# A fused two-layer graph network kernel: the order of the last transition (third norm, tiles held, first tiles of the last layer)

## The chip, the cores and the metric

The kernel runs on one core of one Trainium2 chip. A core has a matrix engine (TensorE, PE in the profile), three engines for elementwise work (VectorE or DVE, ScalarE or ACT, GpSimd or POOL) and a queue engine that issues transfers (SyncE or SP). Each takes its instructions strictly in the order in which they were written, and waits on semaphores where an operand or a buffer comes from another engine. The metric is the device time of one execution in microseconds, lower is better.

## What is computed

Two layers over a batch of 8 graphs with 2048 nodes and 256 features, all sharing one adjacency matrix. Cut to what matters:

```
# layer 0: attention in 8 chunks of 256 keys, 4 heads of 64, softmax within each chunk, chunks summed
q, k, v = x @ Wq.T + bq, x @ Wk.T + bk, x @ Wv.T + bv
scores  = clip(q . k / 8, -10, 10), and -10 where adj == 0
ctx     = sum over chunks of softmax(scores) @ v
a       = layernorm(ctx @ Wo.T + bo + x) * gamma + beta
x1      = layernorm(x + a)

# layer 1: graph attention, 4 heads of 64
Wh      = x1 @ W
e       = leaky_relu(s_src[i] + s_dst[j], 0.2), and -inf where adj == 0
h       = elu(softmax_j(e) @ Wh)
out     = layernorm(x1 + h)
```

Everything is float32; the masks are kept as 8-bit values.

## The kernel before

The kernel walks the graphs b = 0 to 7. For each it runs layer 0 in 64 slots (4 query blocks of 512 nodes, 2 pairs of heads, 8 chunks), taken two at a time in 32 "pairs" (p = 0 to 31). In the same loop it runs layer 1 of the graph before (`lower`), so that the matrix products of one layer cover the elementwise work of the other. The order on every engine is written by hand; no scheduler moves anything.

**A pair of layer 0.** PE makes four blocks of scores (`unit`, L425, tile `ps`), VectorE clips and masks each (`evict`, L444, tile `pr`), ScalarE takes exp (`exps`, L467), PE multiplies by the values (`product`, L478, tile `pc`), ScalarE copies out (L485), and VectorE and GpSimd normalise and add up (`normalize`, L495 to L504).

**A tile of layer 1.** Each graph has 128 tiles: 8 units (2 halves of the rows, 4 heads) of 16 blocks of nodes. `make` produces one tile of weights `e` with one VectorE instruction (L927), out of a row of source factors, a column `gd` and a mask tile; `use` multiplies it into the accumulators `pa` on PE (L964). A pair with layer 1 beside it uses four tiles. `make` runs two tiles ahead of `use`. A tile of `e` takes a buffer from a pool named in `lower.room`, or from the list `lower.extra` of places that happen to be free (parts of `h1`, `qT`).

**Closing a unit.** After 16 tiles ScalarE copies `pa` out (L986), and `close` carries on in steps that `rest(n)` advances: maximum and reciprocal on VectorE (L1007, L1008), a product on GpSimd (L1013, for the last units) or ScalarE (L1019), exp and relu on ScalarE (L1024, L1025), and a combination on VectorE into `h1` (L1029).

**The last graph, b = 7.** Two things differ. First, layer 1 of graph 6 does not run out with the pairs: the last `LATE` slots (12, so six pairs) run alone, and 24 tiles are held back, to be used one by one in the transition. In the lone pairs one tile each is made ahead (four, from p = 27 on, and one more in the last pair). Second, after the transition layer 1 of graph 7 runs with nothing beside it (`alone`). There every third tile (k % 3 == 2, `by_pool`) is made by ScalarE (L888, L889) and GpSimd (L890) instead of VectorE, up to nine tiles ahead (`make_ahead`), and the rest by VectorE. ScalarE copies the row of each unit to PSUM (`lift`, L856). `weigh` (L777, GpSimd) scales the features of one head.

**The transition** is the list `order` near the end of the graph loop. Work on the nodes is done in four groups of 512 (`Between`). When the pairs end, the third group (`before`) still needs its second norm, and the fourth (`group`) everything: context transposes (`ctx`, L528, L531), output matmuls (`steps[1]`, L631), addition (`steps[2]`, L642), first norm (`group.a`, L545 to L557 and L594), scale and addition (`steps[5]`, L648, L651), second norm (`b2`), store, transposes (`turn_all`, L334, L337) and values (L673, L680, L684). The third group's second norm runs as `again` (L651), `sums` and `squares` on ScalarE (L563, L575), `factors` (four small steps on GpSimd, L587 to L590), `finish` (four applies L594 and a store L656 on ScalarE's queue), transposes and values. Then the factors of the last layer: `fs[0]` maximum (L740, L742, L744), `fs[1]` spread (L748, L755 to L762), `fs[2]` rows (L767, L770, L771, L772, L777), and `coming.start`, which broadcasts the row with 16 matmuls (L786). In the list, `M` makes a tile, `U` uses one, `R` advances a closing by one step; they fill the places where PE would otherwise wait.

SP issues the masks of each tile (`et`, L863), the slabs (L413), the group inputs, and in the transition the 2 MB of masks for the first half of the last layer (L825). Row factors (`srow`, L222) are issued in four pieces, one with each `make`, while layer 1 runs beside a pair, and at once otherwise.

Of the kernel before, what the change touches and what calls it, by code (L numbers as in the profile page):

```python
# [18 lines left out]
CH = 512  # L19
# [3 lines left out]
def adj_resnorm_kernel(  # L23
# [19 lines left out]
    nc = tc.nc  # L43
# [26 lines left out]
    PAIRS = SLOTS // 2  # L70
# [2 lines left out]
    FIRST = [sum(BANKS[:m]) for m in range(len(BANKS))]  # L73
    TILES = len(UNITS) * NT
    STEP = TILES // SLOTS
    LATE = 12
    WIDE = max(BANKS)
    AHEAD_E = 5
    AHEAD_P = 8
# [42 lines left out]
    qT = big.tile([P, KC, N], F32, tag="qT", name="qT")  # L122
# [285 lines left out]
    spare, lone = [1], []  # L408
# [281 lines left out]
    every = tuple(range(QT))  # L690
# [106 lines left out]
    class Layer1:  # L797
# [71 lines left out]
            return self.edge.pop(k)  # L869

        def by_pool(self, k):
            return self.alone and k % 3 == 2

        def make_ahead(self, k):

# [284 lines left out]
    for g in range(NCH):  # L1160
        _, _, keys, values, queries = groups[g]
# [67 lines left out]
    lower = None  # L1229
    for b in range(B):  # L1230
# [8 lines left out]
        group = before = None  # L1239
        for p in range(PAIRS):  # L1240
            s0, s1 = 2 * p, 2 * p + 1
            q, i = p // QP, p % QP
            along = lower if b + 1 < B or s0 < SLOTS - LATE else None
            if b + 1 == B and not along:

                lone[:] = [
                    qT[:, 0, : 2 * CH].rearrange("p (k n) -> p k n", k=2),
                    h1[:, :QT, :].rearrange("p (k t) f -> p k (t f)", k=2),
                ]
                if p == PAIRS - 4:  # L1250
                    lower.extra = [
                        h1[:, QT : 2 * QT, :].rearrange("p t f -> p (t f)"),
                        qT[:, 1, : 2 * CH],
                        qT[:, :, 2 * CH : 3 * CH],
                    ]
            more = p + 1 < PAIRS
            slow[0] = bool(along) and more
            if not slow[0]:
                drip(len(pieces))

            def hook(now, later):
                if group and i in now:
                    now[i](group)
                if before and i in later:
                    later[i](before)

            if p + 2 < PAIRS:
                load_slab(p + 2)
            if i == 0 and q:
                before, group = group, Between(b, q - 1, sd, waug)  # L1270
            if p == PAIRS - 2 and b + 1 < B:
                turns = [project(b + 1, g) for g in range(NCH)]
                turns[0].pop(0)()

            ending = b + 1 == B and not more
            if ending:
                room = kT[:, 0, : QT * F].rearrange("p (t f) -> p t f", f=F)
                last = Between(b, NCH - 1, sd, waug, room)

            hook(FIRST_OF, {})  # L1280
            if i == QP - 1 and q > 1:
                turn_context(q, 0)
            if p:
                normalize(s0 - 1)
            if more:
                us = units_of(p + 1)
                waiting = burst(p + 1)
                evict(*waiting[0][0], waiting[0][1])
                exps(*us[0])
                exps(*us[1])  # L1290
            if along:
                along.rest(1)
                along.make()
                along.use()
                along.make()
            else:
                if more:
                    evict(*waiting[1][0], waiting[1][1])
                    exps(*us[2])
                if not lower and masks.left():  # L1300
                    masks.step()
            if ending:
                last.bias()
                lower.room = prp, "pr"
                lower.make()
            hook(MIDDLE_OF, NEXT_MIDDLE)
            for each in closings:
                each.do(p, "add", "factors")
            if i == 2 and q:
                turn_context(q - 1, 1)  # L1310
            if i == QP - 2 and q < 2:
                turn_context(q, 0)
            product(s0)
            send()
            for each in closings:
                each.do(p, "load")
            if i == 1 and q:
                load_context(b, q - 1, 1)
            if i == QP // 2 + 1:
                load_context(b, q, 0)  # L1320
            if along:
                normalize(s0)
                if more:
                    for us_ps in waiting[1:]:
                        evict(*us_ps[0], us_ps[1])
            elif more:
                evict(*waiting[2][0], waiting[2][1])
                exps(*us[3])
                if lone and p >= PAIRS - 5:
                    lower.rest(1)  # L1330
                    lower.make()
            if i == 0 and q:
                send_context(b, q - 1, 1)
            if i == QP // 2:
                send_context(b, q, 0)
            if along:
                if more:
                    exps(*us[2])
                along.rest(1)
                along.use()  # L1340
                along.make()
                along.use()
                along.make()
                along.use()
            elif ending:
                lower.use()
                normalize(s0, nc.vector)
            else:
                normalize(s0)
                if not lower and masks.left() and (p < QP - 2 or p % 2 == 0):  # L1350
                    masks.step()
            if p == PAIRS - 1 and not ending:
                turns[0].pop(0)()
                group.again()
            product(s1)
            if along and more:
                exps(*us[3])
            hook(LAST_OF, NEXT_LAST)
            hook(FINALLY_OF, NEXT_FINALLY)
            for each in closings:  # L1360
                each.do(p, "sums", "squares", "finish")
# [4 lines left out]
        before = group  # L1366
        gd, fs = factors(b, sd, waug)
        group = None
# [8 lines left out]
        coming = Layer1(b, gd, waug)  # L1377
# [8 lines left out]
        def group_shift():  # L1386
            group.shift()

        early = [
            lambda: before.b2.stats(every),  # L1390
            lambda: None,
            lambda: before.finish(),
            lambda: before.load(ep.tile([P, KC, CH], F32, tag="e", name="x1t") if b + 1 < B else None),
            lambda: before.turn(),
            lambda: before.values((0, 1), parts),
            lambda: before.values((2, 3), parts),
        ]
# [13 lines left out]
        if b + 1 < B:  # L1411
            (k0, v0, q0), (l1, t1, k1, v1, q1), (l2, t2, k2, v2, q2), (l3, t3, k3, v3, q3) = turns
            rest = [lambda: lower.rest(1)] if lower else []
            order = [begin, early[0], *rest, l1, k0, ctx, early[2], v0, steps[0], *rest, steps[1], t1, l2, *rest]
            order += [q0, steps[2], early[3], steps[3], l3, k1, *rest, steps[4], v1, early[4], t2, q1]
            order += [steps[5], k2, steps[6], early[5], early[6], steps[7], coming.begin, v2, t3]
            order += [lambda: [load_slab(p) for p in range(2)], steps[8], steps[9]]
            order += [lambda: k3(fs[0]), fs[1], lambda: q2(fs[2]), coming.start, v3, start_next]
            order += [lambda: [exps(*us) for us in units_of(0)], q3, coming.make, coming.make]
        else:  # L1420


            M, U, R = lower.make, lower.use, lambda: lower.rest(1)
            b2 = lambda: before.b2
            order = [begin, U, U, U, ctx, before.again, M, lambda: b2().sums(every), U, steps[1], M]
            order += [steps[2], lambda: group.a.stats(every), lambda: b2().squares(every)]
            order += [lambda: b2().factors(nc.gpsimd), U, U, U, M, U, M, U, early[2], steps[4]]
            order += [before.turn_all, lambda: coming.load_masks(0), group_shift, M, U, early[5], early[6]]
            order += [steps[5], M, U, R, M, U, M, U, R, steps[6], M, U, steps[7], M, U, R, M, U, steps[8]]
            order += [M, U, steps[9], R, M, U, M, U, R, M, U, fs[0], M, U, fs[1], M, U, fs[2], U]  # L1430
            order += [lambda: coming.start(fs[4])]
            assert sum(p is U for p in order) + 1 == LATE * STEP
            assert sum(p is M for p in order) + 2 + 1 + 4 >= LATE * STEP
        for piece in order:
            send()
            piece()
# [6 lines left out]

    closing, ending = Closing(B - 2, CLOSING_ALONE), Closing(B - 1, ENDING)
    weigh = fs[3]
    for _ in range(STEP):
        lower.make()
    for s in range(SLOTS):
# [55 lines left out]
```

## Time and profile before

| | us |
|---|---|
| median of 3 runs (3559.84 to 3566.21) | 3564.57 |
| the profiled execution, its own time | 3559.92 |
| its span in the profile | 3558.1 |
| PE busy in it | 3499.2 |
| pairs 26 to 31 of the last graph (3297.95 to 3347.45) | 49.50 |
| transition (3347.45 to 3397.46) | 50.01 |
| first 12 tiles of the last layer (3397.46 to 3419.72) | 22.26 |
| the other tiles of the last layer (3419.72 to 3544.30) | 124.58 |

The last four rows are read from PE's timeline: the stages end where the first matmul of the next one starts. Times inside the execution are counted from the start of the span. In the views of single engines a row gives start, length, engine, source line, operation and tiles, the number of instructions merged into the row (x), and in brackets the idle time before it with the instruction that ended it.

### The profile page before, as it was taken

To read this page: it belongs to the slowest core of one execution; us is meant where nothing else is said; L and a number is where in the kernel's file an instruction comes from. 1 tells how busy PE (TensorE), PEld (TensorE's weight loads), DVE (VectorE), ACT (ScalarE), POOL (GpSimd) and SP (SyncE) were. 2 spreads that over 40 slices of the span, in tenths; PEclk is the share of its full clock that TensorE was granted. 3 is DMA by queue.
4 is the path that set the end of the run, shared out by engine and by line. 5 is a ranking of instruction groups with operands and counts; after the bars stand their busy time and mean duration, and the time that the engine had idled before them with its cause. 6 is when DMAs were issued, how large, how long until landed. Compare 5 with 4: busy or idle time off the path is not lost. (4 is left out here: it accounts for less than half of the span.)

```text
span 3558.1 us, 170238 instructions
## 1 busy us (share of the span) xinstructions
PE 3499.2 (98%) x76924; PEld 2605.2 (73%) x76924; DVE 3024.2 (85%) x3630; ACT 2308.5 (65%) x4151; POOL 1429.6 (40%) x1265
## 2 busy tenths in 40 slices
PE   8999999999999999999999999999999999999987
PEld 5666677777777777777777767777677776777677
DVE  5886699987999789996999969999699996999878
ACT  4787456655766666665676656666576665767677
POOL 1555233333433333433343334433343442443567
PEclk9999999999999999999999999999999999999999
DMA  7663333443434434434444334344343434434322
GB/s 178 151 133 79 86 101 101 109 98 105 112 108 109 103 107 116 107 104 90 124 116 112 101 86 124 108 112 104 92 123 110 106 92 111 124 109 117 109 87 68
DMA packets 719271, 385.53 MB, mean 108 GB/s; under 512 B 432976, under 2 KB 678608, under 8 KB 718544
## 3 DMA queue, kind: packets, MB, share of 16 engines
q1 hardware_dynamic: 668544, 340.95, 37.2%
q10 hardware_dynamic: 50000, 33.70, 3.0%
q8 instruction: 601, 9.85, 1.2%
q14 instruction: 126, 1.03, 0.1%
HBM read 317.59 MB, written 56.89 MB: 105 GB/s over the span
## 5 line engine op out<-in xcount | busy, mean ns | idle before, releaser
L467 ACT ACTIVATE pr<-pr 128x1024 f32<-128x1024 f32 x955 | 991.2, 1054 | 426.8 <-DVE pr L444 355.3
L444 DVE SCALAR_TENSOR_TENSOR pr<-ps,slab 128x1024 f32<-128x1024 f32 x955 | 1109.5, 1203 | 88.6 <-PE ps L425 80.6
L927 DVE SCALAR_TENSOR_TENSOR e<-srow,gd,et 128x1024 f32<-128x1024 f32 x893 | 1163.1, 1335 | 4.9
L964 PEld LDWEIGHTS pa<-waug,e 128*64 128x64 f32 x32672 | 996.2, 138 | 196.3 <-issue 170.2
L964 PE MATMUL pa<-waug,e 128*64 128x65 f32 x32672 | 1048.9, 223 | 17.8 <-DVE e L927 11.8
L478 PE MATMUL pc<-vaug,pr 128*64 128x65 f32 x30560 | 978.8, 222 | 0.8 <-DVE pr L444 0.8
L502 POOL TENSOR_TENSOR part<-raw,rd 128x512 f32<-128x512 f32 x446 | 473.6, 1062 | 1213.0 <-DVE rd L495 1208.6
L425 PE MATMUL ps<-qT,kT 64*64 64x512 f32 x8192 | 942.3, 596 | 6.1 <-DVE pr L444 3.7
L478 PEld LDWEIGHTS pc<-vaug,pr 128*64 128x64 f32 x30560 | 935.8, 138 | 15.6 <-DVE pr L444 13.1
L425 PEld LDWEIGHTS ps<-qT,kT 64*64 64x64 f32 x8192 | 286.0, 132 | 484.3 <-issue 271.4
L485 ACT COPY raw<-pc 128x520 f32<-128x520 f32 x512 | 302.8, 591 | 484.3 <-PE pc L478 481.4
L504 POOL TENSOR_TENSOR acc<-acc,part 128x512 f32<-128x512 f32 x446 | 585.6, 1313 | 35.1
L502 POOL TENSOR_TENSOR acc<-raw,rd 128x512 f32<-128x512 f32 x64 | 66.8, 1044 | 360.7 <-DVE rd L495 360.7
L495 DVE RECIPROCAL rd<-raw 128x8 f32<-128x8 f32 x512 | 100.4, 196 | 127.4 <-ACT raw L485 120.7
L673 PE MATMUL pw<-w_sb,x1T 128*64 128x264 f32 (+1 forms) x800 | 122.8, 388 | 0.2 <-ACT x1T L337 0.2
L369 PE MATMUL pp<-xT,wk_sb 128*128 128x512 f32 x256 | 119.2, 606 | 2.9 <-DVE xT L325 1.6
L631 PE MATMUL po<-wo_sb,qT 128*64 128x256 f32 (+1 forms) x912 | 120.6, 379 | 0.0
L369 PE MATMUL pp<-xT,wq_sb 128*128 128x512 f32 x256 | 117.4, 598 | 0.0
L385 PE MATMUL pv<-wv_sb,xT 128*128 128x256 f32 x512 | 116.6, 381 | 0.0
L1019 ACT ACTIVATE sums<-sums,dn 128x64 f32<-128x64 f32 x432 | 113.0, 335 | 0.0
L385 PEld LDWEIGHTS pv<-wv_sb,xT 128*128 128x128 f32 x512 | 95.9, 190 | 20.3 <-issue 7.2
L927 DVE SCALAR_TENSOR_TENSOR e<-rowp,gd,et 128x1024 f32<-128x1024 f32 x86 | 103.8, 1268 | 3.0 <-PE rowp L786 3.0
(167 smaller groups left out, 2563.9 us busy)
## 6 DMA issues: line engine op xcount, KB each, us to landing
et<-edgeD SPq DMA_DIRECT2D x896, 128.0 KB, 2.7
slab<-clipD SPq DMA_DIRECT2D x256, 256.0 KB, 3.7
srow<-rowD SPq DMA_DIRECT2D x252, 128.0 KB, 3.4
x1D<-y ACTq DMA_DIRECT2D x32, 512.0 KB, 2.9
xg<-in_x_dram SPq DMA_DIRECT2D x124, 128.0 KB, 3.2
ctxD<-acc ACTq DMA_DIRECT2D x56, 256.0 KB, 3.6
ctx<-ctxD SPq DMA_DIRECT2D x224, 64.0 KB, 2.9
xp<-in_x_dram SPq DMA_DIRECT2D x224, 64.0 KB, 2.3
```

The costliest lines, as they stand in the source:

```text
L369: nc.tensor.matmul(pps[c], lhsT=w[:, kc, c * P : (c + 1) * P], rhs=st["xT"][:, kc, :], start=(kc == 0), stop=(kc == KC - 1),)
L385: nc.tensor.matmul(pv[:, u, :], lhsT=st["xT"][:, kc, u * P : (u + 1) * P], rhs=wv_sb[:, kc, :], start=(kc == 0), stop=(kc == KC - 1),)
L425: nc.tensor.matmul(ps[z * D : (z + 1) * D, k, :], lhsT=kT[rows, hp, t * P + z * D : t * P + (z + 1) * D], rhs=qT[rows, hp, cols], start=Tr ...
L444: nc.vector.scalar_tensor_tensor(pr, ps, -CLIP, row.unsqueeze(1).to_broadcast([P, 2, CH]), op0=ALU.max, op1=ALU.min,)
L467: nc.scalar.activation(pr, pr, AF.Exp, scale=0.125)
L478: nc.tensor.matmul(pc[z * D : (z + 1) * D, k, to], lhsT=probs[s][u][:, k, i * P + z * D : i * P + (z + 1) * D], rhs=vaug[:, KT * c + u, 2 ...
L485: nc.scalar.copy(raws[s].rearrange("p k i d -> p k (i d)"), pc[:, :, : QT * D1])
L502: engine.tensor_mul(part, raw[:, :, :, :D], rd.to_broadcast([P, 2, QT, D]))
L504: engine.tensor_add(accv, accv, part)
L673: nc.tensor.matmul(pw[z, k, : F + 2 * H], lhsT=self.x1T[:, c, u * P + z.start : u * P + z.stop], rhs=w1_sb[:, c, :], start=(c == 0), stop= ...
L927: nc.vector.scalar_tensor_tensor(e, like(row), self.gd[:, h, j : j + 1], like(self.mask(k)), op0=ALU.max, op1=ALU.mult,)
L964: nc.tensor.matmul(self.pa[i // QT][z * D : (z + 1) * D, i % QT, :], lhsT=block(e, i, z), rhs=self.waug[:, j, h, :], start=(j == 0 and i % ...
```

## The change

`LATE` goes from 12 to 10: the sixth pair from the end gets layer 1 beside it again, five pairs run alone, and 20 tiles are held. Five tiles are still made ahead in the lone pairs, now one in each with two in the third pair from the end (p = 29) and none in the last. Two places in `lower.extra` change their order, and the third group's turned-out buffer (`before.t`, named x1t) is added for the tile of p = 30.

In the transition the third group's sums, squares and factors are written ahead of the fourth's statistics, so that L587 to L590 stand ahead of the fourth's L556 and L557 on GpSimd. The maximum's transposes follow two tiles behind the last values, with no VectorE make between the factor steps, and the rows follow the spread directly. The makes and closing steps are spread anew over the list.

In the last layer tile 2 is made by VectorE instead of ScalarE and GpSimd, so that the first three tiles are all VectorE's, and the closing of the last unit of graph 6 is advanced by four steps (`lower.rest(4)`) before the first tile is made, which puts L1007, L1008, L1013, L1024 and L1025 ahead of the tiles on VectorE, GpSimd and ScalarE, and L1029 behind tile 1 on VectorE.

```diff
-    LATE = 12
+    LATE = 10
...
-            return self.alone and k % 3 == 2
+            return self.alone and k % 3 == 2 and k > 2
...
                     lower.extra = [
                         h1[:, QT : 2 * QT, :].rearrange("p t f -> p (t f)"),
+                        qT[:, :, 2 * CH : 3 * CH],
                         qT[:, 1, : 2 * CH],
-                        qT[:, :, 2 * CH : 3 * CH],
                     ]
+                if p == PAIRS - 2:
+                    lower.extra.append(before.t.rearrange("p c n -> p (c n)"))
...
                 lower.room = prp, "pr"
-                lower.make()
...
-                if lone and p >= PAIRS - 5:
+                if lone:
                     lower.rest(1)
-                    lower.make()
+                    for _ in range(1 + (p == PAIRS - 3)):
+                        lower.make()
...
-            order = [begin, U, U, U, ctx, before.again, M, lambda: b2().sums(every), U, steps[1], M]
-            order += [steps[2], lambda: group.a.stats(every), lambda: b2().squares(every)]
-            order += [lambda: b2().factors(nc.gpsimd), U, U, U, M, U, M, U, early[2], steps[4]]
-            order += [before.turn_all, lambda: coming.load_masks(0), group_shift, M, U, early[5], early[6]]
-            order += [steps[5], M, U, R, M, U, M, U, R, steps[6], M, U, steps[7], M, U, R, M, U, steps[8]]
-            order += [M, U, steps[9], R, M, U, M, U, R, M, U, fs[0], M, U, fs[1], M, U, fs[2], U]
-            order += [lambda: coming.start(fs[4])]
+            order = [begin, U, U, U, ctx, before.again, M, U, lambda: b2().sums(every), steps[1], M]
+            order += [lambda: b2().squares(every), lambda: b2().factors(nc.gpsimd), steps[2]]
+            order += [lambda: group.a.stats(every), U, U, U, early[2], M, U, M, U, steps[4], before.turn_all]
+            order += [lambda: coming.load_masks(0), group_shift, M, U, early[5], early[6], steps[5]]
+            order += [M, U, R, M, U, R, steps[6], M, U, M, steps[7], U, R, M, M, steps[8], R, M, U, R, M, M]
+            order += [steps[9], U, U, fs[0], U, fs[1], fs[2], U, lambda: coming.start(fs[4])]
...
     weigh = fs[3]
+    lower.rest(4)
     for _ in range(STEP):
         lower.make()
```

In the list, `early[2]` is the third group's `finish`, `early[5]` and `early[6]` its values, `steps[4]` the fourth's first apply, `steps[6]` its `finish`, `steps[7]` its transposes, `steps[8]` and `steps[9]` its values.

## The prediction, on record before the changed kernel ran

> **What bounds the kernel now.** I read the page first, to see which engine sets the time.
>
> ```profile
> span 3558.1 us, 170238 instructions
> PE 3499.2 (98%) x76924; PEld 2605.2 (73%) x76924; DVE 3024.2 (85%) x3630; ACT 2308.5 (65%) x4151; POOL 1429.6 (40%) x1265
> ```
>
> TensorE (PE) has 58.9 us idle in the whole span, so an edit gains only where PE waits. The second view is the busy time by stage, cut where PE's timeline shows the edges: the last six pairs, the transition, the opening of the last layer (its first 12 tiles), the rest of that layer.
>
> ```profile
> 3297.95:3347.45 49.50, 49.50 (x1028) 33.56 (x1026) 41.70 (x53) 42.85 (x81) 31.87 (x27) 1.00 0.43 111
> 3347.45:3397.46 50.01, 41.00 (x862) 33.61 (x858) 36.34 (x60) 19.47 (x49) 13.65 (x12) 0.93 0.29 95
> 3397.46:3419.72 22.26, 16.31 (x415) 15.91 (x412) 13.76 (x14) 17.58 (x19) 15.78 (x9) 0.95 0.31 98
> 3419.72:3544.30 124.58, 114.32 (x3723) 111.25 (x3720) 108.36 (x136) 103.43 (x121) 103.85 (x68) 1.00 0.25 76
> ```
>
> Columns: length, busy time of PE, weight loads, VectorE (DVE), ScalarE (ACT), GpSimd (POOL), clock granted to PE. In the pairs PE never waits; in the transition it idles 9.0 us and in the opening 6.0, both below full clock. These two stages are what the diff touches. Third, PE's timeline names the waits (in brackets: idle before, and what ended it).
>
> ```profile
> 3367.13 2.80 PE L334 MATMUL pt<-identf,y 128*128 128x128 f32 x8 [4.49 <-ACT y L594]
> ...
> 3372.02 4.30 PE L673 MATMUL pw<-w_sb,x1T 128*64 128x264 f32 x32 [0.15 <-ACT x1T L337]
> ...
> 3405.77 7.69 PE L964 MATMUL pa<-waug,e 128*64 128x65 f32 x256 [2.45 <-POOL e L890]
> 3416.95 3.31 PE L964 MATMUL pa<-waug,e 128*64 128x65 f32 x64 [3.50 <-DVE e L927]
> ```
>
> The largest, 4.49, waits for the third group's normalised y. GpSimd's and ScalarE's timelines show why that is late:
>
> ```profile
> 3360.26 2.05 POOL L556 TENSOR_TENSOR rs_a<-rs_a,nhalf 128x4 f32<-128x4 f32 x1 [11.60 <-DVE off_a L555]
> ...
> 3362.78 1.08 POOL L587 TENSOR_SCALAR rs_b<-mv_b 128x4 f32<-128x4 f32 x1
> ...
> 3366.24 0.20 POOL L590 TENSOR_TENSOR off_b<-off_b,rs_b 128x4 f32<-128x4 f32 x1
> ```
>
> ```profile
> 3366.48 2.07 ACT L594 ACTIVATE y<-y,off_b,rs_b 128x256 f32<-128x256 f32 x4 [6.27 <-POOL off_b L590]
> ...
> 3369.00 2.07 ACT L594 ACTIVATE y<-y,off_a,rs_a 128x256 f32<-128x256 f32 x4 [0.45 <-ACT y L594]
> ...
> 3413.31 0.63 ACT L1024 ACTIVATE ee<-sums 128x512 f32<-128x512 f32 x1 [0.95 <-POOL sums L1013]
> ```
>
> The third norm (rs_b) queues on GpSimd behind the fourth's (rs_a), which idled 11.60 us until VectorE had its statistics; the third's squares were done at 3357.64. Then the fourth's apply (off_a), ready at 3362.7, sits on ScalarE behind the third's until 3369.0. The 3.50 wait comes from VectorE:
>
> ```profile
> 3414.63 1.07 DVE L1029 SCALAR_TENSOR_TENSOR h<-ee,sums 128x512 f32<-128x512 f32 x1 [6.38 <-ACT sums L1025]
> ```
>
> The closing of the layer before (L1013, L1024, L1025, L1029) runs behind four tile multiplications on GpSimd and five tile pairs on ScalarE, and VectorE's in-order queue stops in front of tile 10.
>
> **The change, part by part.** A tile costs PE about 0.96 us (256 records, eight tiles, in 7.69). Times below are on the clock of the trace before with the end of the pairs held at 3347.45.
>
> *Pairs.* One more pair carries four tiles: +3.8 us of PE there, the same off the transition. VectorE gets four more makes at 1.27 in the pairs, 5.1 on 41.7 busy in then 53.3 us: 88%, so cover exists. Its stalls of 2.19 and 1.36 us for output matmuls lie in just these pairs. The pair three from the end makes two tiles; its next eviction came after 1.00 us of waiting, so 1.27 delays it about 0.3 (bounds 0 and 1.3). I take 0.5 with the row loads and edge loads that now interleave ahead of a slab on SP's queue (each issue 0.3 to 0.5). The reordered rooms and the new one (x1t, read last by VectorE itself) add no wait; the make that leaves the last pair (2.31 us, with GpSimd slowed beside it to 2.30 and 2.15) can free up to 1.0 of the 1.40 us that PE waits at the context's transposes. I take 0.85, bounds 0 and 1.0.
>
> *The third norm ahead.* Context transposes at 3350.85, one tile, output matmuls (3.46) to 3355.9, five tiles to 3360.6. The two copies L986 (0.84) now stand on ScalarE ahead of the context's copy, but wait for a tile ending at 3350.3, and are done before the transposes are: nothing. The addition (1.22) ends at 3351.9; four sums at 0.54 and four squares at 0.64 end at 3356.8, while PE is in the output. GpSimd's four factor steps took 3.46 before (3362.78 to 3366.44); the like four of the last layer (L554 to L557) took 1.83. I take 3.46, the same instructions: 3360.2. Apply to 3362.4, transposes behind it to 3363.4, against 3369.86. PE waits about 1.5 there.
>
> By the Trainium skill (GPSIMD Engine Reference, section 1) GpSimd contends with VectorE instructions that have two SBUF inputs; at the new place VectorE adds from PSUM and takes statistics, so by that rule the four steps cost 1.83 and the sum gains up to 1.6 more. The rows 1.08 here and 0.25 in the last layer fit it.
>
> *The fourth group.* Its pow and product on GpSimd now wait for the third's: 3360.2 plus 2.05, 0.30 and gaps is 3362.65. ScalarE issues the third's store (0.37) ahead of the fourth's apply, as before: apply 3362.9 to 3364.95, against 3371.07. Copy of x1T to 3365.9; the third's values, 3.9, to 3369.8 (1.5 waited, after one tile). VectorE: scale, addition, statistics 4.4 to 3369.4; GpSimd 2.72, ScalarE 2.1, to 3374.5; PE uses three tiles meanwhile and ends the transposes at 3375.5, waiting 1.3 to 2.2. Then tile, values 1.8, tile, values 1.8, two tiles, the transposes of the maximum at 3383.1. The maximum (L740) needs sd at 3382.0 and stands behind one make and the closing L1029 (ready 3380.5): 3382.7, no wait. Tile, spread 3384.3, then rows at 3385.7 directly behind the spread's arithmetic and exp (1.4 waited; a tile hid this before), last tile, row broadcast at 3387.0 instead of 3397.46. Less 3.8 that the pairs took: the transition gains 6.7. Four fewer tiles are why waits of 1.5, 1.5, 2 and 1.4 stay. SP passes four edge loads behind the 2 MB of masks instead of eight, each used five makes later. Bounds: 1.5 (GpSimd and ScalarE steps half as long again and the context wait kept) to 8.5.
>
> *Opening.* Offsets R from the row broadcast. Early closing: last copies of sums at R+0.5, maximum and reciprocal at R+0.9, GpSimd's weighting done R+0.9, L1013 1.04 to 2.08, L1024 and L1025 1.27: R+3.2 to R+4.3. What queues behind is ScalarE's first L888, which needs R+3.88 (3401.34) anyway: 0 to 0.4 late. VectorE makes tiles 0, 1 (R+2.1 to R+4.5), L1029 0.65, then 2, 3, 4 at 1.2 each: R+6.4, 7.6, 8.8. PE meets tile 5, GpSimd's first, at R+9.8; it is done at R+8.3, where tile 2 was before. From there PE runs on at 0.97: tile 12 at R+16.6 to 16.8 against R+22.26. Gain 5.5: the 2.45 and 3.50 waits and about 1.2 of slow clock (64 records in 3.31 against 1.95), less 1.2 for tiles 2 to 4 and rests. ScalarE's and GpSimd's lanes move with it (one tile of 2.2 less each, closing out of the way), so I carry all; lower bound 0, if they bind the 124.58 us that follow; upper bound 6.
>
> By the Trainium skill (TensorE: Matmul & The Clock Gate, Part 1) an idle window of about 3.4 us halves the clock until PE has been busy as long; the trace agrees: 2.45 (and 2.53 later) kept 1.00, 3.50 and 4.49 did not. Its figures make each such loss an estimated 1.7 us, by which the sum would change by under one.
>
> **Sum.** 6.7 + 5.5 - 0.5 = 11.7, I forecast 11.5: the profiled 3559.92 would be 3548.4. Its time is the lowest but one of those shown; from the median 3564.57 the forecast is 3553.
>
> **Rivals.**
> 1. *The last layer's lanes take back the opening.* For: ScalarE is 98% busy from 3460 to 3500. Against: it waited for PE or GpSimd in between. Gain 0 there, 6.7 less 0.5 before it: 3558.4.
> 2. *The stall only moves on*: the fourth's chain stays as long as before (24.7 us from output to the end of its transposes, 19.6 in mine) with four tiles less cover. For: GpSimd's pow 2.05 comes later in its queue. Against: 6.3 of it was queueing on ScalarE. The transition gains about 1, the opening 5.5: 3558.
> 3. *The other side*: the same chain grows past before. Place: fourth norm's pow, apply, and second pow; each step held by VectorE's makes and the store ahead. PE's idle grows with it one for one, and two waits pass 3 us and cost some 3 us of slow clock each, as the 4.49 did (transposes 2.80 against 1.09, a tile 2.0 against 0.96). From 25.1 us of chain on the gain is gone; at 32 it is 12.4 + 6 - 11.5 = 7 slower, 3571. For: nothing but fewer tiles. Against: every step has a row above.
> 4. *The change does not do what it says*: L1029, now third in VectorE's queue, waits as before. It would need L1013 late by over 3 us, and nothing is ahead of it but the weighting. Gain 7 to 8, inside the forecast's range.
>
> **How the numbers follow.** Forecast 0.67 (with 4), rival 1 0.13, rival 2 0.12, rival 3 0.08. A measurement of this kernel can tell about 0.2%, 7 us, from no change. Rivals 1 and 2 fall inside that, so faster 0.67, same 0.25, slower 0.08. The runs of before spread 6.4 us. Low end: the upper bounds (8.5 and 6) and a low run, 3546; high end: rivals 1 and 2 with a high run, 3562. The forecast's own range is 3547 to 3557.
>
> **What would show it.** Right: rs_b's L587 starts before rs_a's L556; L594 off_b ends about 4 to 6 us earlier against the end of the pairs; no PE wait over 3 us between the pairs and tile 12; clock 1.00 there; tile 12 about 16.8 us behind the broadcast; L1029 with almost no wait. Wrong: PE waits in the pairs; a wait over 3 us at the fourth's transposes; the rest of the last layer longer than 124.58 by more than 2.

## The result and the profile after

The changed kernel takes 3553.23 us (median of 10 runs, 3552.13 to 3557.01). Beside it the kernel before took 3561.2 (10 runs, 3559.07 to 3566.21). The ratio is 0.9977 with a 95% interval of 0.9968 to 0.9987: 8.0 us faster. The interval leaves out 1, but the difference is hardly more than the 0.2% that the forecast took as the least that can be told from no change. The profiled execution took 3554.9, against 3559.92. First its page, the span and the busy time of the engines:

```profile
span 3553.1 us, 170247 instructions
PE 3496.8 (98%) x76924; PEld 2605.4 (73%) x76924; DVE 3033.1 (85%) x3631; ACT 2306.8 (65%) x4149; POOL 1426.0 (40%) x1264
```

Then the same four stages as before, by windows (length, busy time of PE, weight loads, VectorE, ScalarE, GpSimd, clock, DMA share, GB/s):

```profile
3299.84:3352.65 52.81, 52.81 (x1156) 37.05 (x1154) 46.26 (x57) 43.11 (x81) 31.15 (x27) 1.00 0.43 113
3352.65:3392.81 40.16, 34.18 (x735) 28.14 (x731) 31.49 (x55) 19.25 (x49) 11.91 (x12) 1.00 0.32 104
3392.81:3409.50 16.69, 16.05 (x433) 15.51 (x431) 15.47 (x15) 14.35 (x16) 12.32 (x8) 1.00 0.43 131
3409.50:3539.30 129.80, 113.63 (x3707) 111.01 (x3701) 115.64 (x136) 104.37 (x122) 104.65 (x68) 0.96 0.24 73
```

The third window reaches half a tile past the twelfth: it has 433 matmuls, the like stretch of the kernel before 415. In the changed kernel the 415th is reached at 3409.00, 16.19 behind the broadcast, and the table goes by that.

| stage | before | after | difference | forecast |
|---|---|---|---|---|
| start of pair 26 | 3297.95 | 3299.84 | +1.89 | 0 |
| pairs 26 to 31 | 49.50 | 52.81 | +3.31 | +4.3 |
| transition | 50.01 | 40.16 | -9.85 | -10.5 |
| first 12 tiles of the last layer | 22.26 | 16.19 | -6.07 | -5.5 |
| rest of the last layer | 124.58 | 130.30 | +5.72 | 0 |
| tail | 13.80 | 13.80 | 0 | 0 |

The first row arises ahead of the changed code, so it belongs to this pair of executions and not to the change. Pairs and transition together gave 6.54. The opening gave 6.07 and the rest of the last layer took 5.72 of it back, at a lower clock (0.96 against 1.00). PE's timeline shows where:

```profile
3356.85 0.63 PE L528 MATMUL pt<-identf,acc 128*128 128x128 f32 x4 [1.23 <-DVE acc L504]
...
3367.60 1.09 PE L334 MATMUL pt<-identf,y 128*128 128x128 f32 x8
3371.91 3.78 PE L673 MATMUL pw<-w_sb,x1T 128*64 128x264 f32 x32 [2.14 <-ACT x1T L337]
...
3399.22 22.52 PE L964 MATMUL pa<-waug,e 128*64 128x65 f32 x744 [0.56 <-DVE e L927]
...
3436.34 10.06 PE L964 MATMUL pa<-waug,e 128*64 128x65 f32 x288 [8.46 <-DVE e L927]
```

The transposes that waited 4.49 and then ran 2.80 (granted clock 0.50 from 3367.13 to 3371.00) now wait for nothing and run 1.09. The opening's 2.45 and 3.50 are gone: from 3399.22 PE runs 22.5 us on end. Then comes one new wait of 8.46 us. All engines around it:

```profile
3423.98 2.37 POOL L1067 TENSOR_TENSOR h<-h,kT 128x1024 f32<-128x1024 f32 x1
...
3425.38 9.72 DVE L1029 SCALAR_TENSOR_TENSOR h<-ee,sums 128x512 f32<-128x512 f32 x1 [4.13 <-ACT sums L1025]
3426.32 3.96 POOL L890 TENSOR_TENSOR e<-e,et 128x1024 f32<-128x1024 f32 x2
...
3430.25 2.34 POOL L1067 TENSOR_TENSOR h<-h,kT 128x1024 f32<-128x1024 f32 x1
...
3432.55 1.99 POOL L890 TENSOR_TENSOR e<-e,et 128x1024 f32<-128x1024 f32 x1
...
3435.02 2.46 DVE L927 SCALAR_TENSOR_TENSOR e<-rowp,gd,et 128x1024 f32<-128x1024 f32 x2
```

L1029 closes unit 0. Alone it takes 0.68 us (the closing of graph 6, at 3397.28); here its row is 9.72 long. It starts 1.40 us into an addition on GpSimd and ends at 3435.10, 0.56 behind the last of five GpSimd instructions that follow each other without a gap. VectorE makes no tile in that time, and PE runs out of them. In the kernel before, the same instruction asked at the same point:

```profile
3434.22 2.38 POOL L1067 TENSOR_TENSOR h<-h,kT 128x1024 f32<-128x1024 f32 x1
...
3435.63 1.52 DVE L1029 SCALAR_TENSOR_TENSOR h<-ee,sums 128x512 f32<-128x512 f32 x1 [3.33 <-ACT sums L1025]
3436.56 4.46 POOL L890 TENSOR_TENSOR e<-e,et 128x1024 f32<-128x1024 f32 x2
```

It asked 1.41 us into L1067, ran at the next boundary, and GpSimd's two L890 took 4.46 instead of 3.96. So the hold is not the price of meeting GpSimd as such. Even the changed kernel shows that: at unit 4 L1029 asks 1.32 us into an L1067 with an L890 directly behind it, and is in at the boundary between them:

```profile
3500.45 1.62 DVE L1029 SCALAR_TENSOR_TENSOR h<-ee,sums 128x512 f32<-128x512 f32 x1
```

The chain of waits of the changed kernel has the hold as its longest piece, and gives it no name (start, length, what):

```profile
3425.52 9.50 issue
3435.02 2.46 DVE e L927 x2
```

"Issue" is time for which the profile shows no releaser. Here it lies inside L1029's own row: no late semaphore is shown, the instruction itself is long.

### The profile page after: what moved, and what is told of

Its sections match the earlier page's. It is cut to its first block, busy times and chain, and to the rows that moved or that the text cites. A ratio compares the mean times of both kernels' runs of the same rounds, so it can differ in the third digit from the quotient of the medians.

```text
span 3553.1 us, 170247 instructions
## 1 busy us (share of the span) xinstructions
PE 3496.8 (98%) x76924; PEld 2605.4 (73%) x76924; DVE 3033.1 (85%) x3631; ACT 2306.8 (65%) x4149; POOL 1426.0 (40%) x1264
## 3 DMA queue, kind: packets, MB, share of 16 engines
q8 instruction: 601, 9.85, 1.1%
## 5 line engine op out<-in xcount | busy, mean ns | idle before, releaser
L927 DVE SCALAR_TENSOR_TENSOR e<-srow,gd,et 128x1024 f32<-128x1024 f32 x892 | 1161.3, 1335 | 5.0
L927 DVE SCALAR_TENSOR_TENSOR e<-rowp,gd,et 128x1024 f32<-128x1024 f32 x87 | 104.9, 1269 | 0.7 <-PE rowp L786 0.7
```

The source lines that it names most:

```text
L927: nc.vector.scalar_tensor_tensor(e, like(row), self.gd[:, h, j : j + 1], like(self.mask(k)), op0=ALU.max, op1=ALU.mult,)
```

## Experiments

Three groups ran, each with runs of the kernel before on the same chip (medians 3563.63 of 26, 3565.37 of 11, 3562.76 of 9), so ratios are compared and not microseconds. The table has two lengths read from PE's timeline of each profile: from the context transposes L528 to the row broadcast L786, and from the broadcast to the end of the last tile. Both are from one execution each. The start of the first length differs by up to 7 us between kernels that are alike up to there (3354.86 to 3361.93); the lengths differ less. With the changed transition the first is 35.96 to 36.04, but 34.86 or 34.87 in e5, e9 and e10, which do not touch the transition: there L557 of the fourth group's first norm took 0.31 to 0.32 instead of 1.45 at the same place. Some 1.1 us of those three is therefore not due to their edits.

| run | ratio | interval | transposes to broadcast | last layer | L1029 of unit 0 |
|---|---|---|---|---|---|
| before | 1 | | 45.64 | 146.83 | 1.52 |
| the change | 0.9977 | 0.9968 to 0.9987 | 35.96 | 146.53 | 9.72 |
| e1, no new opening | 0.9980 | 0.9970 to 0.9989 | 35.97 | 145.22 | 1.53 |
| e2, new opening alone | 0.9996 | 0.9987 to 1.0005 | 45.96 | 147.30 | 9.73 |
| e3, additions later | 0.9961 | 0.9948 to 0.9973 | 35.96 | 138.46 | 1.17 |
| e4, third norm back | 0.9991 | 0.9982 to 1.0000 | 41.44 | 147.25 | 9.72 |
| e5, additions on VectorE | 0.9957 | 0.9945 to 0.9970 | 34.86 | 140.27 | 1.16 |
| e6, longer row (one run) | | | 35.96 | 147.77 | 11.61 |
| e7, tile 2 as before | 0.9969 | 0.9958 to 0.9980 | 36.04 | 149.37 | 9.70 |
| e8, e3 and a product on VectorE | 0.9952 | 0.9938 to 0.9966 | 37.54 | 138.26 | 1.17 |
| e9, a short set between | 0.9965 | 0.9952 to 0.9978 | 34.86 | 142.66 | 1.51 |
| e10, a short product between | 0.9958 | 0.9944 to 0.9972 | 34.87 | 142.35 | 1.53 |

**e1: the change without its new opening.**

```diff
-            return self.alone and k % 3 == 2 and k > 2
+            return self.alone and k % 3 == 2
...
-    lower.rest(4)
```

> The changed kernel with the opening of the last layer as before: tile 2 by ScalarE and GpSimd again, no closing ahead of the tiles; pairs and transition stay changed. Theory (the stages add; the transition is worth 6.5 us, the opening 5.6, and 5.2 of that is lost again where VectorE's L1029 of the first unit is held for 9.72 us): about 3554.5, some 1 us above the changed kernel, with the waits of 2.45 and 3.50 us back in the opening, no hold over 2 us in the first unit's L1029, and the row broadcast as early as in the changed kernel. Rival (the opening is what gains, the transition moves a wait only): 3558 to 3561.

The opening's waits are back (2.45 for GpSimd's tile, 1.93), L1029 isn't held, and the ratio is that of the whole change. Within the intervals the transition carries all of the time that the change wins.

**e2: the kernel before with the new opening alone** (the same two edits the other way round).

> The kernel before with the changed opening alone: tile 2 by VectorE and the closing advanced by four steps ahead of the tiles. Theory (stages add, and the hold comes from how ScalarE's and GpSimd's lanes stand to each other after the row broadcast, which is the same as in the changed kernel): tile 12 about 16.7 us behind the broadcast, the first unit's L1029 held 8 to 10 us again, time 0 to 1 below before, about 3560.5. Rival (the hold is an accident of one execution): 5 us below before, 3556. Rival (the lanes bind the last layer whatever happens): 3560.5 with no hold, the idle time of PE spread over many waits.

The interval holds 1. PE runs on from 3406.84, 6.4 us behind the broadcast at 3400.43, as in the changed kernel, and then meets the hold:

```profile
3432.98 9.73 DVE L1029 SCALAR_TENSOR_TENSOR h<-ee,sums 128x512 f32<-128x512 f32 x1 [4.01 <-ACT sums L1025]
...
3443.97 1.34 PE L964 MATMUL pa<-waug,e 128*64 128x65 f32 x19 [8.16 <-DVE e L927]
```

The hold therefore needs only the new opening, not the new transition.

**e3: graph 6's additions later.** L1067 adds the residual for two groups of graph 6; it is wanted late. The steps "pool", "stats" and "finish" move back by some slots, and GpSimd's row is broken.

```diff
-        10: [(2, "pool")],
-        13: [(3, "pool")],
-        14: [(2, "stats")],
-        17: [(3, "stats"), (2, "finish")],
-        20: [(3, "finish")],
+        15: [(2, "pool")],
+        18: [(2, "stats")],
+        21: [(2, "finish")],
+        23: [(3, "pool")],
+        26: [(3, "stats")],
+        29: [(3, "finish")],
```

> The changed kernel with graph 6's two additions on GpSimd (L1067, 2.4 us each) moved from slots 10 and 13 of the last layer to slots 15 and 23, and their statistics and finishes behind them, so that GpSimd's row of L1013, L1067, L890, L890, L1067, L890 without a gap is broken up. Theory (VectorE, which needs two SBUF operands in L1029, gets in only when GpSimd's unbroken row of instructions ends): GpSimd then waits for ScalarE's tile behind two or three tiles, the first unit's L1029 takes under 4 us instead of 9.72, PE's wait of 8.46 shrinks to under 3, and the time falls by 4 to 7 us, to 3546 to 3549. Rival (the lanes take back the opening anyway): L1029 short, time within 1.5 us of the changed kernel. Rival (L1029 waits for the additions themselves, which write the same tensor): L1029 takes as long or longer.

```profile
3427.64 2.05 POOL L890 TENSOR_TENSOR e<-e,et 128x1024 f32<-128x1024 f32 x1
...
3429.07 1.17 DVE L1029 SCALAR_TENSOR_TENSOR h<-ee,sums 128x512 f32<-128x512 f32 x1 [3.49 <-ACT sums L1025]
3431.40 2.01 POOL L890 TENSOR_TENSOR e<-e,et 128x1024 f32<-128x1024 f32 x1 [1.71 <-ACT e L889]
```

L1029 again asks 1.4 us into a GpSimd instruction, but behind that one GpSimd waits 1.71 us for ScalarE, and VectorE gets in. The last layer falls by 8.07 us against the changed kernel and its largest wait is 1.72. The ratio is clear of 1; its interval still touches that of the changed kernel. The median of 3550.04 lies 1 us above the times expected.

**e4: the third norm back behind the fourth's statistics**, all else as changed.

```diff
-            order += [lambda: b2().squares(every), lambda: b2().factors(nc.gpsimd), steps[2]]
-            order += [lambda: group.a.stats(every), U, U, U, early[2], M, U, M, U, steps[4], before.turn_all]
+            order += [steps[2], lambda: group.a.stats(every), lambda: b2().squares(every)]
+            order += [lambda: b2().factors(nc.gpsimd), U, U, U, early[2], M, U, M, U, steps[4], before.turn_all]
```

> The changed kernel with the third norm's squares and factors written behind the fourth's statistics again, so that on GpSimd L556 and L557 of the fourth stand ahead of L587 to L590 of the third; all else stays. Theory (the third norm's place on GpSimd is what the transition gained from): the third's apply L594 starts about 5 us later against the end of the pairs, PE waits over 4 us at the third's transposes and loses clock, the fourth's apply queues behind it, and the time rises by 4 to 7 us, to 3557 to 3560. Rival (the smaller hold of 20 tiles and the two makes moved into the pairs made the gain): within 1.5 us of the changed kernel.

GpSimd, and PE behind it:

```profile
3363.67 2.06 POOL L556 TENSOR_TENSOR rs_a<-rs_a,nhalf 128x4 f32<-128x4 f32 x1 [11.61 <-DVE off_a L555]
...
3367.33 1.14 POOL L587 TENSOR_SCALAR rs_b<-mv_b 128x4 f32<-128x4 f32 x1
...
3370.86 2.80 PE L334 MATMUL pt<-identf,y 128*128 128x128 f32 x8 [4.80 <-ACT y L594]
```

The old picture returns: GpSimd idles 11.61 us, the third norm queues behind the fourth, PE waits 4.80 and then needs 2.80 for the transposes instead of 1.09. The transition is 5.48 longer than with the change, of the 9.68 that it won there (some 3.8 of which are the four tiles that the pairs took over). Moving the third norm is thus nearly all of the rest, 5.48 of some 5.9.

**e5: the additions on VectorE**, in the old slots.

```diff
-        10: [(2, "pool")],
-        13: [(3, "pool")],
+        10: [(2, "add")],
+        13: [(3, "add")],
...
-            each.do(s, "load", "pool", "stats", "most", "finish")
+            each.do(s, "load", "pool", "stats", "most", "finish", *(["add"] if each is closing else []))
```

> The changed kernel with graph 6's two additions made by VectorE (1.2 us each) in their old slots instead of GpSimd, the run without additions on GpSimd then being L1013 and L890 only. Theory (VectorE is held until GpSimd's unbroken row ends): the first unit's L1029 takes under 4 us, PE's wait there under 3, time 3 to 6 us below the changed kernel, a little above the run with the additions moved later, since VectorE carries 2.4 us more. Rival (moving the additions later helped by something else, for instance the finishes on ScalarE coming later): L1029 short but the time within 1.5 us of the changed kernel.

L1029 takes 1.16, the wait at its place is 2.06 (the additions cost VectorE 1.85 and 2.14), and the time is that of e3 within the intervals. So the later slot isn't needed: it is enough that GpSimd's row is broken.

**e6: a longer row.** GpSimd's scaling of the fourth head (`weigh`, L777) moves from slot 9 to slot 13, into the row.

```diff
-        if s % QT == 1 and s // QT + 1 < H:
-            weigh(s // QT + 1)
+        if s in (1, 5, 13):
+            weigh((1, 5, 13).index(s) + 1)
```

> The changed kernel with the weighting of the fourth head (L777, 1.92 us on GpSimd) moved from slot 9 to slot 13, so that L1013 comes 1.9 us earlier and the weighting stands inside the unbroken row, ahead of the second addition. Theory (VectorE gets in only when the row ends): VectorE asks 1.9 us earlier, the row ends at the same place, so L1029 takes about 11.6 us instead of 9.72 and ends about 0.55 us behind the last GpSimd instruction of the row. Rival (the hold belongs to L1067, by its tensor or its length): L1029 takes 4 to 8 us, or ends behind the second L1067. Rival (a fixed time-out): 9.72 again.

```profile
3423.07 11.61 DVE L1029 SCALAR_TENSOR_TENSOR h<-ee,sums 128x512 f32<-128x512 f32 x1 [1.92 <-ACT sums L1025]
3423.99 4.01 POOL L890 TENSOR_TENSOR e<-e,et 128x1024 f32<-128x1024 f32 x2
3427.93 1.95 POOL L777 TENSOR_TENSOR waug<-waug,ed 128x1024 f32<-128x1024 f32 x1
3429.81 2.36 POOL L1067 TENSOR_TENSOR h<-h,kT 128x1024 f32<-128x1024 f32 x1
3432.11 2.02 POOL L890 TENSOR_TENSOR e<-e,et 128x1024 f32<-128x1024 f32 x1
```

One instruction of 1.95 more in the row, and the hold is 1.89 longer. It ends at 3434.68, 0.55 behind the row. In this execution too the hold ends with GpSimd's row, and not a fixed time after VectorE asked.

**e7: tile 2 made by ScalarE and GpSimd again, the early closing kept** (the first edit of e1 alone).

> The changed kernel with tile 2 made by ScalarE and GpSimd as before, the closing still ahead of the tiles. Theory (the two halves of the opening remove one wait each, and the hold needs lanes that run ahead): the wait of 2.45 us for GpSimd at tile 2 is back or larger (its lane starts behind L1013), the 3.50 is not; tile 12 about 19 us behind the broadcast; time between the changed kernel and 3 us above it if the hold is there again, 3 us below if it is not. Rival (tile 2 adds nothing): tile 12 at 16.7 us.

Tile 2 is late again (PE waits 2.46), tile 12 comes 17.5 us behind the broadcast where 19 was expected, and the hold is there (9.70), so the early closing alone brings it. The time can't be told from the changed kernel's, where up to 3 us more was expected: this edit's part is under the noise. The profiled execution is this kernel's longest run (3562.91), so its 149.37 is not used.

**e8: e3, and the product L557 of the fourth group on VectorE in the transition.** In the changed kernel that product took 1.45 us on GpSimd where 0.20 is its cost undisturbed.

```diff
-                nc.gpsimd.tensor_mul(self.off, self.off, self.rs)
+                (nc.vector if quick[0] else nc.gpsimd).tensor_mul(self.off, self.off, self.rs)
...
+        quick[0] = b + 1 == B
```

> The kernel with the additions moved later, and in the transition the last product of the fourth group's two norms (L557) on VectorE instead of GpSimd, where VectorE waits for the pow and so leaves GpSimd alone for it. Theory (the fourth group's chain now sets the transition, and its pow takes 2.04 us only because VectorE's makes run beside it, 1.04 when alone): pow near 1.05 twice, the product 0.2 instead of 1.45 and 0.59, the fourth's transposes end 2 to 3 us earlier against the end of the pairs, time 1.5 to 3 us below the run with the additions moved later. Rival (makes that VectorE starts later cost PE as much in its tiles): within 1 us of that run.

A miss for the transition. Both pows take 1.01 instead of 2.04, but VectorE now waits for them in its queue, in front of tiles:

```profile
3372.33 1.15 PE L966 MATMUL pa<-waug,e 128*64 128x65 f32 x32 [1.99 <-DVE e L929]
...
3382.66 3.62 PE L966 MATMUL pa<-waug,e 128*64 128x65 f32 x64 [2.34 <-DVE e L929]
```

The transition grows from e3's 35.96 to 37.54. Much of that is clock: behind the wait of 2.34 PE was granted 0.53, and 64 matmuls took 3.62. The ratio of 0.9952 can't be told from e3's 0.9961 or e5's 0.9957.

**e9 and e10: one short instruction behind each addition.** In e9 it sets the 128x4 column `nhalf` once more to the value it has; in e10 it multiplies `nhalf` by itself into a new tile.

```diff
+            if each is closing and s in (10, 13):
+                nc.gpsimd.memset(nhalf, -0.5)
```

```diff
+    scr = consts.tile([P, QT], F32, tag="scr", name="scr")
...
+            if each is closing and s in (10, 13):
+                nc.gpsimd.tensor_tensor(scr, nhalf, nhalf, ALU.mult)
```

> The changed kernel with one short GpSimd instruction more behind each of the two additions L1067: it sets the 128x4 column nhalf to -0.5 once more, and reads nothing from SBUF. Open so far: L1029 asks 1.4 us into L1067, and got in at the next boundary in the kernel before (1.52 us), but not with the early closing (9.72). If GpSimd keeps VectorE out only from one instruction with two SBUF inputs straight to the next, the short set is a door: L1029 takes 1.2 to 1.7 us, PE's wait of 8.46 falls under 3, and the time is that of the kernel with the later additions (0.9961). If any unbroken row holds, whatever its instructions, L1029 takes 9.8 to 10.1 (9.72 and the short instruction) and the ratio stays at 0.9977. In between: it is let in behind the second addition's set only, 8 us.

> The same place, but the short instruction is a product of nhalf with itself into a new 128x4 tile: two SBUF inputs, and as short (L557, the like one, took 0.20 us). If only an instruction without two SBUF inputs opens the row, L1029 is held for 9.9 to 10.1 us and the ratio stays at 0.9977. If one more boundary is enough, whatever stands there, 1.2 to 1.7 us and 0.996. If the short product is itself slowed beside the waiting VectorE (1.08 against 0.25, as L587 was in the kernel before), it takes about 1 us and L1029 is still held.

All engines at the place, in e9:

```profile
3427.52 2.38 POOL L1067 TENSOR_TENSOR h<-h,kT 128x1024 f32<-128x1024 f32 x1
...
3428.94 1.51 DVE L1029 SCALAR_TENSOR_TENSOR h<-ee,sums 128x512 f32<-128x512 f32 x1 [4.15 <-ACT sums L1025]
3429.84 0.11 POOL L1460 MEMSET nhalf<- 128x4 f32 x1
3429.90 4.41 POOL L890 TENSOR_TENSOR e<-e,et 128x1024 f32<-128x1024 f32 x2
```

and in e10, whose lines are numbered one higher:

```profile
3424.31 2.37 POOL L1068 TENSOR_TENSOR h<-h,kT 128x1024 f32<-128x1024 f32 x1
...
3425.71 1.53 DVE L1030 SCALAR_TENSOR_TENSOR h<-ee,sums 128x512 f32<-128x512 f32 x1 [3.91 <-ACT sums L1026]
3426.65 0.65 POOL L1461 TENSOR_TENSOR scr<-nhalf 128x4 f32<-128x4 f32 x1
```

Either one is enough: VectorE asks 1.42 and 1.40 us into the addition, as in the changed kernel, and is in at its end. The short product, which reads SBUF, opens the row as well as the set, which reads nothing; it pays 0.65 instead of the 0.19 that the second one took (3433.55). GpSimd still has no idle time there. L1029 therefore did not wait for the additions to be done, nor only for GpSimd to be idle. The last layer falls to 142.66 and 142.35. The intervals of both ratios (0.9965 and 0.9958) still overlap that of the changed kernel, so the gain over it rests on one profiled execution each.

## Why the prediction was right, and where it was not

The forecast was 3553 and the measurement 3553.23. That they meet so closely is luck. The forecast is a gain of 11.5 from the first three runs' median of 3564.57; the ten runs taken beside the change have 3561.2, so the gain is 8.0. A base 3.4 too high and a gain 3.5 too large cancelled. The part for pairs and transition was sound (6.2 forecast, 6.54 measured); the part for the opening was not.

- *Pairs*: four tiles and the double make were to cost 4.3; 3.31 came, PE did not wait, and VectorE was busy 46.26 of 52.81, the 88% foreseen. The 0.5 for the double make and SP's queue was not needed; why it is less than the 3.8 of the four tiles alone is open.
- *Third norm*: confirmed. L587 stands ahead of L556 and its apply starts 12.07 us behind the end of the pairs instead of 19.03, 7.0 earlier where "about 4 to 6" was named (the working's own times give 6.1). PE waited for nothing at the transposes behind it, where 1.5 was forecast. The surplus is GpSimd's four steps:

```profile
3362.74 0.24 POOL L587 TENSOR_SCALAR rs_b<-mv_b 128x4 f32<-128x4 f32 x1 [9.06 <-ACT junk L575]
...
3364.48 0.20 POOL L590 TENSOR_TENSOR off_b<-off_b,rs_b 128x4 f32<-128x4 f32 x1
3365.28 2.04 POOL L556 TENSOR_TENSOR rs_a<-rs_a,nhalf 128x4 f32<-128x4 f32 x1 [0.60 <-DVE off_a L555]
3367.41 1.45 POOL L557 TENSOR_TENSOR off_a<-off_a,rs_a 128x4 f32<-128x4 f32 x1
```

They took 1.94 (3362.74 to 3364.68), not the 3.46 that I kept (the rows of before even give 3.66, from 3362.78 to 3366.44). The like steps of the last layer, with 1.83, were the better price. By the Trainium skill's rule (GPSIMD Engine Reference, section 1) that was the price to expect, and the trace agrees with it here.
- *Fourth group*: its pow L556 waited 0.60 for VectorE's statistics and not, as forecast, for the third's steps. Its product L557 took 1.45 where I had 0.30 (and where e5, e9 and e10 had 0.31 to 0.32), so its apply came 16.24 behind the pairs (forecast 15.45), ScalarE waiting for GpSimd for 2.09 before it:

```profile
3364.72 2.08 ACT L594 ACTIVATE y<-y,off_b,rs_b 128x256 f32<-128x256 f32 x4 [2.06 <-POOL off_b L590]
3368.89 2.08 ACT L594 ACTIVATE y<-y,off_a,rs_a 128x256 f32<-128x256 f32 x4 [2.09 <-POOL off_a L557]
```

PE waited 2.14 at the third's values (forecast 1.5), 0.31 at the fourth's transposes (1.3 to 2.2) and 1.09 at the rows (1.4); the context's wait fell only from 1.40 to 1.23, not by 0.85 (which would have been 3350.97 and not the working's 3350.85). The broadcast came 40.16 behind the pairs, forecast 39.55. No wait passed 3 us and the clock stayed at 1.00. That a wait under 3 us costs no clock does not hold in the other runs, though: behind waits of 2.45 (e1), 2.34 (e8) and 2.14 (e7) PE was granted 0.55, 0.53 and 0.68 in the 3.5 to 5.4 us that followed, where the 2.45 of the kernel before kept 1.00. The length of one wait doesn't decide it.
- *Opening*: tile 12 came 16.2 behind the broadcast (forecast 16.6 to 16.8), both of its long waits were gone, and L1029 of graph 6 ran without waiting. Confirmed.
- *The step that failed* is "so I carry all". I asked only whether ScalarE's and GpSimd's lanes would keep up. They did, but L1029 of unit 0 was held on VectorE for 9.72 us beside GpSimd's row. The term +5.5 was worth 0.3 over the whole last layer (146.83 to 146.53). Its lower bound of 0 covered that size, but for another reason, lanes that bind. This is also the sign named for a wrong forecast: the rest of the last layer is longer by more than 2.
- *Rivals*: the size of rival 1 (the last layer takes the opening back) is what happened, by another mechanism than the lanes it named. Had the lanes bound, e9 and e10 could not have ended the last layer 4.2 and 4.5 us earlier than before with nothing but a short instruction more. (The row for ScalarE from 3460 to 3500 reads 97%, not 98.) Rivals 2 and 3 fell with the fourth's chain at 19.1 (from the end of the output matmuls to the end of its transposes; 24.7 before, 19.6 in the forecast), rival 4 with L1029's 0.68.

The cause of the hold is shown as far as this: it ends with GpSimd's row (e6), goes when that row is broken (e3, e5) or gets one short instruction more (e9, e10), comes with the new opening alone (e2), and of its two edits the early closing is enough (e7). Open is why the boundary from L1067 to L890 let VectorE in before and in e1 and not in the five kernels with the early closing and that row: the instructions, their order and the moment of asking (1.40 to 1.43 us into L1067) are the same. At unit 4 the same two instructions meet L1029 in all twelve executions, and it took 1.10 to 1.63 each time, so the pair alone doesn't shut it out. How far ahead ScalarE's tile for that L890 was done doesn't decide either: 1.82 and 2.00 us before L1067 began in the two that let VectorE in, 2.43 to 2.73 in four that held it, but 0.36 in e6, which held it as well. Each kernel has one execution here, so chance in a single execution isn't ruled out for any one of them. Whether in e9 and e10 the shortness of the instruction or the shifted place of all behind it opens the row was not tried apart.

## What to carry to other kernels

A stage that gains must be followed to the end of the program: here 6.1 us were won at the start of the last layer, and 5.7 of them were lost again 16 us later on another engine. When a faster start closes the gaps of GpSimd's queue, look for VectorE instructions with two operands in SBUF beside it: move GpSimd work that is wanted late out of the dense stretch, give it to VectorE, or break the row with a short instruction, each of which was worth 4 to 8 us of the last layer in the execution profiled here. An instruction whose row is many times its usual length, with "issue" in the chain of waits, was here the sign to look at what another engine did in that time, and not for a late semaphore.

## What the runs showed of the hardware

A VectorE instruction of 0.68 us whose two operands (`ee`, `sums`) lie in SBUF was held for 9.72 and 11.61 us by GpSimd instructions of 1.9 to 2.4 us each that followed one another without a gap, and ended 0.55 to 0.56 us behind the last. L927, which reads its row from PSUM, ran at 1.2 us beside GpSimd instructions of the same kinds (six in 7.19 from 3414.05, beside L890 and L777).

The Trainium skill (SBUF — State Buffer, "SBUF: two separate sides" and "Who interferes with whom") says that the two engines share one pair of ports as an exclusive lock, that a VectorE instruction with two SBUF inputs contends with a GpSimd instruction that reads SBUF, and that the one who comes first has the pair for its whole instruction. By that the hold would end with L1067: an estimated 0.97 (2.37 less 1.40) and 0.68, 1.65 in all. The 1.52 of before and the 1.51 and 1.53 of e9 and e10 agree; the 9.72 and 11.61 do not, and the measurement decides. If it is this lock that held L1029, which no trace shows as such, GpSimd kept it over four and five boundaries between its instructions.

With a set of 128x4 values, 0.11 us on GpSimd, that changes nothing in the data, the last layer was 3.9 us shorter (146.53 to 142.66, one execution each).

A wait of PE of 2.45 us left the granted clock at 1.00 in the kernel before and was followed by 0.55 in e1 (over the next 3.73 and 3.78 us).
